# Group norm's chain spread over single-engine steps, fp8 rounding shared with GpSimd, and a searched start order

## The chip, the cores and the metric

The kernel runs on one NeuronCore of one Trainium2 chip. The metric is the device time of one execution in microseconds, the median of several runs. The engines are named as the profile names them: PE (matmul), PEld (its weight loads), DVE (VectorE), ACT (ScalarE), POOL (GpSimd) and SP (SyncE, which issues most DMAs here).

## The reference, cut to what matters

Two layers act on an image batch `x` of shape (4, 64, 64, 96). Layer 0 is a group norm over the image, a layer norm over the channels, one wide projection and a linear scan along the 4096 positions of each image, for 96 channels with 16 states each. Layer 1 is attention without a softmax (so that it collapses into one 96x96 matrix for each image) and a feed-forward net with values rounded to fp8 (e5m2) ahead of both products.

```python
x = x + conv(_gn(x))          # layer 0
t = t + attn(_ln_t(t))        # layer 1: (q k^T) v, no softmax
t = t + ffn(_ln_t(t))         # rounded to fp8 before each product

def _gn(v, G=32, eps=1e-5):   # 32 groups of 3 channels, over a whole image
    m = jnp.mean(g, axis=(1, 2, 4), keepdims=True)
    s = jnp.var(g, axis=(1, 2, 4), keepdims=True)
    return ((g - m) / jnp.sqrt(s + eps)).reshape(v.shape)

def step(h, ins):             # layer 0, over 4096 positions
    h_new = d * (A_t * h) + d * (B_t * u_t[..., None])
    y = g_t * jnp.sum(C_t * h_new, axis=-1)
```

## The kernel before, in words

Each of the 4 images is cut into 8 chunks of 512 positions, and each chunk's 1536 rows of state into 12 tiles of 128 partitions. That makes 384 tiles, numbered k, and the main loop (L1401 to L1424) makes one **step** s for each. In step s it emits, in this order: for tile s+3 the projection B on PE (`b_proj`, three matmuls, L269) and its copy out of PSUM on ACT (`b_copy`, L811); the projections A of tile s+1 and C of tile s on PE; `keep` on ACT; the product `b_mul` of tile s+2 on POOL (L814); on some tiles `c_mul_pool` of tile s-1 on POOL (L863); on DVE the scan of tile s (L830), `a_mul` of tile s+1 (L823) and `c_mul` of tile s (L854). Then it emits what `call(s)` finds in a table of other work for this step. Engines run what they are given in the order in which it was emitted, each engine for itself, and wait for one another through semaphores. Projection B has one PSUM bank, A two, and the small products share three banks named M.

The table is filled by `at(step, fn)`. The offsets of a chunk's pieces are in the dictionary `AT`. `front` puts the layer norm and the projections of the next chunks there, `tail` and `ffn` the second layer of earlier ones, and `group_norm` the statistics of the next image: `sums` and `sums_out` for its 8 chunks, and then a chain of small pieces. `moments` (L579) is two DVE and three POOL instructions; `mean` (L588) is a matmul, two DVE instructions and two on POOL; `root` (L600) is a matmul, one DVE instruction and one on POOL; `diagonal` (L608) is on ACT; `spread` (L616) is a matmul, and `spread_out` (L623) an ACT copy of the result to all partitions. `make` (L632) opens the group norm of an image with `first` (L561), a transpose and ACT instructions (L564, L566); image b's `make` is in step 6 for b = 1, in step 63 for b = 2 and in step 159 for b = 3, so the next image's `make` falls near the end of an image's chain. The last `sums` of images 1, 2 and 3 are in steps 57, 149 and 245.

Before step 6 and after step 383 the order comes from a small **planner** (class `Plan`, L412). A `job` has an engine, a cost in microseconds, a function that emits its instructions and the jobs it comes after. The planner places jobs by time and rank; with `tries` above zero it repeats that with random changes of rank and keeps the order whose `late` value is the lowest. It only fixes the order in which instructions are emitted; on the chip the instructions wait for their real inputs. `planned_start` (L1222) plans the first nine tiles and the normalization of the first two chunks, with `tries` at 0. The plan `end` (L888, 800 tries) orders what is left after the last step: the second layer of the last image and the last feed-forward chunks of the image before it, 11 chunks' feed-forward in all.

In the end a feed-forward chunk goes through `attention` (PE), `residual` and `stats` (DVE), `rstd` (POOL, L378 and L392), `apply` (ACT at L396, or DVE at L403 where `vector` is set), `transpose` (PE), `quant_in` (ACT, L1098), three `hidden` (PE, L1102) with `round_hidden` (ACT, L1119) and `relu_vector` (DVE, L1123), `quant` (ACT, L1127: 128x1536 values from fp16 to fp8), `project_out` (PE, L1133), `round_out` (ACT at L1143 or DVE at L1141), `bias_out` and `total` (POOL at L1148 and L1155, or DVE), and `store` (SP).

## Time and profile before

| what | value |
|---|---|
| median of 3 runs | 1183.2 us (1182.86 to 1183.66) |
| the profiled execution's own time | 1184.49 us |
| its span, first to last instruction | 1182.8 us |
| busy: PE, DVE, POOL, ACT | 1140.1, 1113.2, 1030.3, 817.3 us |
| first scan begins (tile 0) | 34.74 us |
| scan of tile 6 begins (first step of the loop) | 53.34 us |
| last scan begins (tile 383) | 1108.38 us |

The span is 1.69 us shorter than the time of that execution, and that execution is 1.29 us above the median. A line of a timeline reads: start, duration, engine, source line, operation, output and input with their sizes, count, and in brackets the idle time of the engine just before, with the instruction that ended it. A merged line (x4) covers several instructions in a row. A line of the table by stretches gives the stretch, its length, the busy time of each engine with its count of instructions, the granted PE clock, the busy share of the DMA engines and GB/s.

### The profile page before, as it was taken

To read this page: it belongs to the slowest core of one execution; us is meant where nothing else is said; L and a number is where in the kernel's file an instruction comes from. 1 tells how busy PE (TensorE), PEld (TensorE's weight loads), DVE (VectorE), ACT (ScalarE), POOL (GpSimd) and SP (SyncE) were. 2 spreads that over 40 slices of the span, in tenths; PEclk is the share of its full clock that TensorE was granted. 3 is DMA by queue.
4 is the path that set the end of the run, shared out by engine and by line. 5 is a ranking of instruction groups with operands and counts; after the bars stand their busy time and mean duration, and the time that the engine had idled before them with its cause. 6 is when DMAs were issued, how large, how long until landed. Compare 5 with 4: busy or idle time off the path is not lost. (4 is left out here: it accounts for less than half of the span.)

```text
span 1182.8 us, 19203 instructions
## 1 busy us (share of the span) xinstructions
PE 1140.1 (96%) x5899; PEld 874.6 (74%) x5899; DVE 1113.2 (94%) x2093; ACT 817.3 (69%) x1826; POOL 1030.3 (87%) x1176
## 2 busy tenths in 40 slices
PE   5999999999999999999999999999999999999885
PEld 4777777677777777777777777777777777777573
DVE  6999999899999999999999999999999999999865
ACT  4666655556556777877877777777776777776476
POOL 5798887788889899999999999999999999988554
PEclk8999999899999999999999999999999999999989
DMA  7676776687776776787777777766777778667221
GB/s 185 142 167 143 167 155 154 141 176 161 170 160 151 161 162 157 158 190 170 161 159 161 172 162 166 171 158 152 159 165 169 160 162 185 147 145 153 60 75 47
DMA packets 104288, 182.12 MB, mean 154 GB/s; under 512 B 42637, under 2 KB 50769, under 8 KB 104186
## 3 DMA queue, kind: packets, MB, share of 16 engines
q1 hardware_dynamic: 90060, 106.96, 37.3%
q0 software_dynamic: 13536, 73.93, 31.4%
q8 instruction: 46, 0.75, 0.3%
q14 instruction: 56, 0.46, 0.1%
q10 hardware_dynamic: 590, 0.02, 0.0%
HBM read 69.12 MB, written 24.77 MB: 79 GB/s over the span
## 5 line engine op out<-in xcount | busy, mean ns | idle before, releaser
L814 POOL TENSOR_TENSOR bu<-bu,rep 128x512 f32<-128x512 f32 x384 | 512.9, 1345 | 43.3 <-ACT state L840 34.8
L830 DVE TENSOR_TENSOR_SCAN h<-Aps,state,bu 128x512 f32<-128x512 f32 x336 | 426.2, 1268 | 0.7 <-POOL ch L863 0.5
L811 ACT ACTIVATE bu<-Bps,b_bac 128x512 f32<-128x512 f32 x384 | 263.1, 685 | 198.5 <-PE Bps L269 192.9
L823 DVE SCALAR_TENSOR_TENSOR Aps<-Aps,b_bac,rep 128x512 f32<-128x512 f32 x384 | 281.9, 734 | 8.2 <-PE Aps L269 8.2
L269 PE MATMUL Bps<-xs,w 128*128 128x512 f32 x768 | 268.0, 430 | 7.7 <-ACT bu L811 7.1
L269 PE MATMUL Aps<-xs,w 128*128 128x512 f32 x768 | 242.2, 396 | 1.2 <-DVE h L830 1.0
L863 POOL TENSOR_TENSOR ch<-ch,h 128x512 f32<-128x512 f32 x126 | 170.4, 1352 | 7.9 <-ACT ch L860 3.7
L269 PEld LDWEIGHTS Aps<-xs,w 128*128 128x128 f32 x768 | 143.9, 188 | 37.3 <-DVE h L830 3.0
L269 PEld LDWEIGHTS Bps<-xs,w 128*128 128x128 f32 x768 | 126.7, 191 | 51.2 <-ACT bu L811 15.4
L269 PE MATMUL Aps<-xl,w 128*128 128x512 f32 x384 | 152.0, 396 | 0.0
L269 PE MATMUL Bps<-xl,w 128*128 128x512 f32 x384 | 151.7, 395 | 0.0
L269 PE MATMUL Dps<-xs,w 128*128 128x512 f32 x384 | 121.0, 396 | 0.0
L269 PE MATMUL Cps<-xs,w 128*128 128x512 f32 x384 | 120.6, 395 | 0.0
L854 DVE SCALAR_TENSOR_TENSOR ch<-Dps,b_bac,h 128x512 f32<-128x512 f32 x160 | 118.6, 742 | 0.9 <-PE Dps L269 0.5
L869 POOL DMA_DIRECT2D ch<-ch x94 | 89.6, 953 | 0.3 <-DMA ch<-ch 0.3
L269 PEld LDWEIGHTS Bps<-xl,w 128*128 128x128 f32 x384 | 72.5, 189 | 17.7
L269 PEld LDWEIGHTS Dps<-xs,w 128*128 128x128 f32 x384 | 72.3, 188 | 17.7
L269 PEld LDWEIGHTS Aps<-xl,w 128*128 128x128 f32 x384 | 72.2, 188 | 17.7
L269 PEld LDWEIGHTS Cps<-xs,w 128*128 128x128 f32 x384 | 72.0, 188 | 17.6
L860 ACT ACTIVATE ch<-Cps,b_bac 128x512 f32<-128x512 f32 x94 | 64.6, 688 | 24.1 <-PE Cps L269 24.1
L269 PE MATMUL Dps<-xl,w 128*128 128x512 f32 x192 | 75.9, 395 | 0.0
L269 PE MATMUL Cps<-xl,w 128*128 128x512 f32 x192 | 75.8, 395 | 0.0
(200 smaller groups left out, 2045.2 us busy)
## 6 DMA issues: line engine op xcount, KB each, us to landing
ch<-ch POOLq DMA_DIRECT2D x94, 768.0 KB, 6.7
rep<-ddd SPq DMA_DIRECT2D x124, 384.0 KB, 7.4
ddd<-dd SPq DMA_DIRECT2D x31, 384.0 KB, 3.2
xl<-lo SPq DMA_DIRECT2D x62, 128.0 KB, 2.5
x<-in_x_dram SPq DMA_DIRECT2D x32, 192.0 KB, 3.0
xatd<-xat SPq DMA_DIRECT2D x32, 192.0 KB, 3.6
xal<-xatd SPq DMA_DIRECT2D x32, 192.0 KB, 2.8
out_dram<-o SPq DMA_DIRECT2D x32, 192.0 KB, 2.1
```

What stands on the lines that cost most here:

```text
L269: nc.tensor.matmul(ps, lhsT=wt[:, n], rhs=mv, start=(n == 0), stop=(n == 2))
L811: nc.scalar.activation(self.bu, self.b_ps, AF.Identity, bias=self.bias(0))
L814: nc.gpsimd.tensor_tensor(self.bu, self.bu, rep[self.b, self.i][:, 1, self.cg], ALU.mult)
L823: nc.vector.scalar_tensor_tensor(self.a_ps, self.a_ps, self.bias(1), rep[self.b, self.i][:, 0, self.cg], ALU.add, ALU.mult,)
L830: nc.vector.tensor_tensor_scan(self.h, self.a_ps, self.bu, 0.0 if self.i == 0 else state[self.sh, self.cg], ALU.mult, ALU.add,)
L854: nc.vector.scalar_tensor_tensor(self.slot(), self.c_ps, self.bias(2), self.h, ALU.add, ALU.mult)
L860: nc.scalar.activation(self.ch, self.c_ps, AF.Identity, bias=self.bias(2))
L863: nc.gpsimd.tensor_tensor(self.ch, self.ch, self.h, ALU.mult)
L869: nc.gpsimd.dma_start(chs[g, 0], chs.pop((g, sh)), accum_op=ALU.add)
```

## The change

Six edits. **Group norm's chain**: `moments`, `mean` and `root` are cut into seven pieces (`moments`, `variances`, `group_sums` twice, `mean`, `squares`, `offset`, `root`), each of which issues to one engine, and the eleven pieces of the whole chain are put one a step from the step after the last `sums_out`; before, the chain lay in 5 steps, with the last piece 8 steps after the last `sums`, and now it ends 12 steps after it. **Weights**: the four `weights_` functions emit their PE transposes in one step and their DVE copies in the next. **The end**: `quant` runs on POOL for chunks with i % 3 other than 0; `round_out` runs on ACT for all chunks; `apply` runs on DVE for i % 4 == 0 where it was i % 2 == 0 (last image); 1500 tries. **The fetch** of image 2's last chunk goes from step K - 4 to K - 1. **The second chunk's centring** on POOL comes after the first split (`low`) on POOL, where it waited for a time mark. **The start** is searched, with 800 tries, for a low weighted sum of end times: half the weight on the last planned scan, half on the second chunk's read, 0.01 on every other job.

```diff
--- before.py
+++ after.py
@@ -334,23 +334,26 @@
     def weights_attention():
         ps = bank("M", [C, CA], "wq_ps")
         nc.tensor.transpose(ps, w_qkv[:, 0:C], ident[:CA, :CA])
-        nc.vector.tensor_copy(w_qt[0:C, :], ps)
+        return lambda: nc.vector.tensor_copy(w_qt[0:C, :], ps)
 
     def weights_ffn1():
         ps = bank("M", [C, HID], "w1_ps")
         for m in range(NK):
             nc.tensor.transpose(ps[:, m * P : (m + 1) * P], w1_sb[:, m, :], ident)
-        nc.vector.tensor_copy(w1_q, ps, saturate=False)
+        return lambda: nc.vector.tensor_copy(w1_q, ps, saturate=False)
 
     def weights_ffn2():
         ps = bank("M", [P, NK, C], "w2_ps")
         for m in range(NK):
             nc.tensor.transpose(ps[:, m, :], w2_sb[:, m * P : (m + 1) * P], ident[:C, :C])
-        nc.vector.tensor_copy(w2_q, ps, saturate=False)
+        return lambda: nc.vector.tensor_copy(w2_q, ps, saturate=False)
 
     def weights_bias():
         ps = bank("M", [P, NK], "b1_ps")
         nc.tensor.transpose(ps, b1_sb, ident[:NK, :NK])
+        return lambda: biases_out(ps)
+
+    def biases_out(ps):
         b1_8 = small.tile([P, NK], F8, tag="b1_8", name="b1_8", bufs=1)
         nc.vector.tensor_copy(b1_8, ps, saturate=False)
         nc.vector.tensor_copy(b1_q, b1_8)
@@ -520,7 +523,9 @@
                 self.time[e] = t + j["cost"]
 
         def late(self, starts):
-            return max(t + self.jobs[n]["cost"] for n, t in starts.items())
+
+            ends = [(t + self.jobs[n]["cost"], self.jobs[n].get("weight", 0.0)) for n, t in starts.items()]
+            return sum(t * w for t, w in ends) or max(t for t, _ in ends)
 
     steps = {}
 
@@ -580,29 +585,45 @@
             t = small.tile([C, 2], F32, tag="gt", name=f"gt_{self.b}", bufs=2)
             nc.vector.tensor_reduce(t, self.s, AX.X, ALU.add)
             nc.vector.tensor_scalar_mul(t, t, 1.0 / L)
+            self.t = t
+
+        def variances(self):
+            t = self.t
             nc.gpsimd.tensor_tensor(self.mv[:, 0:1], t[:, 0:1], self.c, ALU.subtract)
             nc.gpsimd.tensor_tensor(t[:, 0:1], t[:, 0:1], t[:, 0:1], ALU.mult)
             nc.gpsimd.tensor_tensor(self.mv[:, 1:2], t[:, 1:2], t[:, 0:1], ALU.subtract)
 
 
+        def group_sums(self, name):
+            self.ps = bank("M", [C, 2], f"g{name}_ps_{self.b}")
+            nc.tensor.matmul(
+                self.ps[:, 0:1], lhsT=third, rhs=self.mv[:, 0:1] if name == "m" else self.w,
+                start=True, stop=True,
+            )
+
         def mean(self):
-            ps = bank("M", [C, 2], f"gm_ps_{self.b}")
-            nc.tensor.matmul(ps[:, 0:1], lhsT=third, rhs=self.mv[:, 0:1], start=True, stop=True)
+            ps = self.ps
             self.m = small.tile([C, 2], F32, tag="gm", name=f"gm_{self.b}", bufs=2)
             nc.vector.tensor_copy(self.m[:, 0:1], ps[:, 0:1])
             w = small.tile([C, 1], F32, tag="gw", name=f"gw_{self.b}", bufs=2)
             nc.vector.tensor_tensor(w, self.mv[:, 0:1], ps[:, 0:1], ALU.subtract)
-            engine = nc.gpsimd if self.b else nc.vector
+            self.w = w
+
+        def squares(self):
+            w, engine = self.w, nc.gpsimd if self.b else nc.vector
             engine.tensor_tensor(w, w, w, ALU.mult)
             engine.tensor_tensor(w, w, self.mv[:, 1:2], ALU.add)
-            self.w = w
+
+        def offset(self):
+            self.v = small.tile([C, 1], F32, tag="gv", name=f"gv_{self.b}", bufs=2)
+            nc.vector.tensor_scalar(self.v, self.ps[:, 0:1], 1e-5, None, ALU.add)
 
         def root(self):
-            ps = bank("M", [C, 2], f"gv_ps_{self.b}")
-            nc.tensor.matmul(ps[:, 0:1], lhsT=third, rhs=self.w, start=True, stop=True)
-            v = small.tile([C, 1], F32, tag="gv", name=f"gv_{self.b}", bufs=2)
-            nc.vector.tensor_scalar(v, ps[:, 0:1], 1e-5, None, ALU.add)
-            nc.gpsimd.tensor_tensor(self.m[:, 1:2], v, mhalf[0:C, 0:1], ALU.pow)
+            nc.gpsimd.tensor_tensor(self.m[:, 1:2], self.v, mhalf[0:C, 0:1], ALU.pow)
+
+        def all_of(self, *pieces):
+            for name, *args in pieces:
+                getattr(self, name)(*args)
 
 
         def diagonal(self, k0=0, k1=2):
@@ -649,9 +670,12 @@
                 at(max(when[n] - 7, when[n - 1]), load_gx, b, n)
             at(when[n], call, "sums", n)
             at(when[n] + AT["sums_out"] - AT["sums"], call, "sums_out", n)
-        for n, name in ((1, "moments"), (2, "mean"), (4, "root"), (6, "diagonal"), (8, "spread"),
-                        (8, "spread_out")):
-            at(when[-1] + n, call, name)
+        chain = (
+            ("moments",), ("variances",), ("group_sums", "m"), ("mean",), ("squares",),
+            ("group_sums", "v"), ("offset",), ("root",), ("diagonal",), ("spread",), ("spread_out",),
+        )
+        for n, args in enumerate(chain):
+            at(when[-1] + AT["sums_out"] - AT["sums"] + 1 + n, call, *args)
 
 
     split, rep, gate = {}, {}, {}
@@ -891,7 +915,7 @@
         {"ACT": 0.5, "DVE": 2.5, "POOL": 1.5},
     )
     end.last = {}
-    end.tries = 800
+    end.tries = 1500
 
     def place(plan, s0):
 
@@ -1064,7 +1088,7 @@
         def tile_of(tag, drain_tag, shape, dtype, name):
             return sb(drain_tag if phase["end"] else tag, shape, dtype, f"{name}_{nm}")
 
-        vector = b == B - 1 and i % 2 == 0
+        vector = b == B - 1 and i % 4 == 0
 
         def fetch():
             v["xa"] = next_of(xal_t, "xal")
@@ -1124,7 +1148,10 @@
 
         def quant():
             v["hq"] = sb("bu", [P, NK, TC], F8, f"hq_{nm}")
-            nc.scalar.activation(v["hq"], v["h16"], AF.Copy, saturate=False)
+            if i % 3 == 0:
+                nc.scalar.activation(v["hq"], v["h16"], AF.Copy, saturate=False)
+            else:
+                nc.gpsimd.tensor_copy(v["hq"], v["h16"], saturate=False)
 
         def project_out():
             ps = v["ps"] = bank("A" if phase["end"] else "M", [P, J, C], f"y2_ps_{nm}")
@@ -1137,10 +1164,7 @@
 
         def round_out():
             v["y16"] = tile_of("y16", "xs", [P, J, C], F16, "y16")
-            if phase["end"] and i % 2:
-                nc.vector.tensor_copy(v["y16"], v["ps"])
-            else:
-                nc.scalar.copy(v["y16"], v["ps"])
+            nc.scalar.copy(v["y16"], v["ps"])
 
         def bias_out():
             last_two = phase["end"] and b == B - 1 and i > NCH - 3
@@ -1170,7 +1194,7 @@
         )
         done = place(plan, s0)
         if fetch not in done and b < B - 1:
-            at(K - 4, fetch)
+            at(K - 1, fetch)
             done.add(fetch)
         if store in done:
             return
@@ -1203,10 +1227,10 @@
                         free=[f"h:{nm}"] if m == 2 else [])
                 c = job("ACT", 0.57, round_hidden, m, after=[h, c],
                         take=[f"rep:{nm}"] if m == 0 else [], free=[f"M:{m}{nm}"])
-                r.append(job("DVE", 0.5, relu_vector, m, after=[c]))
-            a = job("ACT", 1.5, quant, after=r, take=[f"bu:q{nm}"], free=[f"rep:{nm}"])
+                r.append(job("DVE", 0.47, relu_vector, m, after=[c]))
+            a = job(*(("ACT", 1.5) if i % 3 == 0 else ("POOL", 1.6)), quant, after=r, take=[f"bu:q{nm}"], free=[f"rep:{nm}"])
         a = job("PE", 0.5, project_out, after=[a], take=[f"A:y{nm}"], free=[f"bu:q{nm}"])
-        a = job(*(("ACT", 0.48) if vector else ("DVE", 0.56)), round_out, after=[a],
+        a = job("ACT", 0.48, round_out, after=[a],
                 take=[f"xs:{nm}"], free=[f"A:y{nm}"])
         last_two = b == B - 1 and i > NCH - 3
         a = job(*(("DVE", 0.6) if last_two else ("POOL", 0.95)), bias_out, after=[a], take=[f"xl:{nm}"], free=[f"xs:{nm}"])
@@ -1243,8 +1267,8 @@
         b = mm(0.8, bias_turn, after=[b], key="M:b")
         b = job("DVE", 0.35, bias_out, after=[b], free=["M:b"])
         a = job("DVE", 0.4, q.aggregate, after=a)
-        m = job("DVE", 1.1, q.mean, after=[a])
-        r = job("DVE", 0.7, q.root, after=[m], late=0.9)
+        m = job("DVE", 1.1, q.all_of, ("group_sums", "m"), ("mean",), ("squares",), after=[a])
+        r = job("DVE", 0.7, q.all_of, ("group_sums", "v"), ("offset",), ("root",), after=[m], late=0.9)
         g = []
         for n, a in enumerate((m, r)):
             a = job("ACT", 0.37, q.diagonal, n, n + 1, after=[a, *g])
@@ -1260,6 +1284,7 @@
         wd = job("SP", 1.0, split_copies, w_dug[:, 0], w_dug[:, 1], w_dug[:, 2], after=[ld], late=2.2)
         wr = [job("ACT", 0.45, repeat, n, k, after=[(hd, ld)[n]]) for n in range(2) for k in range(2)]
         w = {"rep": job("SP", 1.0, split_copies, *(w_rep[:, n] for n in range(3)), after=wr, late=2.2)}
+        first_low = None
         for sh in range(NSH):
             plan.rank = 3 * sh - 3
             for k in range(3):
@@ -1270,6 +1295,7 @@
                     plan.rank = 1 if k == 0 else 3 * sh - 3
                     t = job("POOL", 1.3, low, k, sh, nc.gpsimd, after=[t, calm])
                     low_b = t if k == 0 else low_b
+                    first_low = first_low or t
                 v = w_bac[k][:, :, :, sh * P : (sh + 1) * P]
                 w[k, sh] = job("SP", 1.0, split_copies, *(v[:, n] for n in range(3)), after=[t], late=2.4)
         plan.rank = -4
@@ -1325,7 +1351,7 @@
 
 
         plan.rank = 1
-        a = job("POOL", 1.0, second.centre, nc.gpsimd, after=[*g, calm])
+        a = job("POOL", 1.0, second.centre, nc.gpsimd, after=[*g, first_low])
         a = job("POOL", 1.0, second.scale, nc.gpsimd, after=[a])
         a = job("DVE", 1.1, second.stats, after=[a])
         a = job("POOL", 1.8, second.ln.rstd, after=[a])
@@ -1345,7 +1371,7 @@
         b = mm(0.7, second.proj, 0, after=[a], key="M:u2")
         a = job("DVE", 0.74, second.du_out, after=[a, b], free=["M:u2"])
         a = job("SP", 0.5, second.write, after=[a], late=3.4)
-        job("SP", 1.8, second.read, after=[a])
+        read = job("SP", 1.8, second.read, after=[a])
         plan.rank = 6
         job("SP", 0.5, load_gx, 1, 0, after=[land("free0", 34.0)])
         job("SP", 4.0, load_late, after=[land("free1", 37.0)])
@@ -1362,13 +1388,22 @@
                 awake[0][:, 0:P], lhsT=ident, rhs=ident, start=True, stop=True
             )
 
+
+        for j in plan.jobs:
+            j["weight"] = 0.01
+        for j in (s, read):
+            j["weight"] = 0.5
+        plan.tries = 800
         plan.run(stay_awake)
         return second
 
     second = planned_start()
 
+    def turned(step, fn):
+        at(step + 1, fn())
+
     for n, fn in enumerate((weights_attention, weights_ffn1, weights_ffn2, weights_bias)):
-        at(NT + 8 + NT * n, fn)
+        at(NT + 8 + NT * n, turned, NT + 8 + NT * n, fn)
     for b in range(B):
         for i in range(NCH):
             g = b * NCH + i
```

## The prediction

> **What bounds the kernel now.** I read the busy shares first, then the busy times by stretch, then the timelines of single engines where DVE or PE stands idle.
>
> ```profile
> PE 1140.1 (96%) x5899; PEld 874.6 (74%) x5899; DVE 1113.2 (94%) x2093; ACT 817.3 (69%) x1826; POOL 1030.3 (87%) x1176
> ...
> 53.34:1108.40 1055.06, 1044.17 (x5307) 804.11 (x5305) 1025.38 (x1849) 740.26 (x1690) 963.64 (x1074) 1.00 0.73 160
> 1108.40:1125.50 17.10, 15.26 (x110) 9.77 (x110) 11.71 (x48) 8.78 (x18) 6.57 (x12) 1.00 0.23 67
> 1125.50:1142.00 16.50, 16.48 (x97) 13.40 (x97) 10.53 (x48) 9.72 (x17) 8.80 (x15) 0.69 0.29 86
> 1142.00:1174.20 32.20, 23.62 (x201) 16.18 (x198) 21.39 (x75) 30.67 (x52) 17.09 (x24) 1.00 0.18 49
> ```
>
> The columns are PE, PEld, DVE, ACT, POOL, then PE's clock. In the loop (first stretch) DVE and PE run level. Adding up every idle time in DVE's timeline between 44 and 1107 us gives 28.4 us, of which 17.1 is one wait of 0.2 to 1.0 us in each chunk (L926, for `o_ps`), which no edit touches. In the last stretch ACT is busy 30.67 of 32.20 us: there ACT is the bound, and POOL has 15 us free. Between these two lies a latency chain (last scan, gram matrix, attention matrix at 1125.4).
>
> The largest stop in the loop is at image 1's group norm, on ACT:
>
> ```profile
> 212.07 1.54 ACT L396 ACTIVATE z<-z,nmr_c,rstd_c 128x96 f32<-128x96 f32 x4 [1.53 <-POOL nmr_c L384]
> 213.51 0.63 ACT L612 ACTIVATE gdg<-ident,gm 96x96 f32<-96x96 f32 x2
> 214.05 0.58 ACT L564 ACTIVATE gc_ps<-gc_ps 96x512 f32<-96x512 f32 x1
> ...
> 214.88 0.67 ACT L811 ACTIVATE bu<-Bps,b_bac 128x512 f32<-128x512 f32 x1
> ```
>
> on PE:
>
> ```profile
> 215.61 1.22 PE L269 MATMUL Bps<-xs,w 128*128 128x512 f32 x2 [2.56 <-ACT bu L811]
> ```
>
> and on DVE:
>
> ```profile
> 218.57 0.76 DVE L823 SCALAR_TENSOR_TENSOR Aps<-Aps,b_bac,rep 128x512 f32<-128x512 f32 x1 [2.42 <-PE Aps L269]
> ```
>
> A late layer norm, the group norm's diagonal (L612) and the next image's `make` (L564) meet in step 63. They hold back the copy L811 that frees PE's only B bank; PE stands 2.56 us and then works at half speed:
>
> ```profile
> 216.00:221.00 5.00, 5.00 (x16) 3.98 (x15) 2.06 (x4) 1.08 (x3) 2.57 (x3) 0.50 0.78 191
> ```
>
> [...] Here 2.56 us was enough (clock 0.50), while 1.90 us of idle PE at 1144.08 left the next stretch at 1.00; the measurement decides. [...] L403 takes 0.32 us undisturbed, and up to 1.22 us in the start beside POOL (below).
>
> **The change, part by part.** The sum is made against the profiled execution, 1184.49 us (span 1182.8), which is 1.29 above the median; I subtract the same sum from the median 1183.2.
>
> *Group norm, image 1.* DVE's idle times at 214.87, 218.57, 219.85 and 223.03 are 0.53 + 2.42 + 0.52 + 1.24 = 4.71 us. The diagonal moves from step 63 to 67, which takes 0.55 us (start to start, L612 to L564) out of ACT's burst. `root` (0.58 us on POOL, L605) leaves step 61, so the layer norm's rstd and then L396 begin about 0.55 earlier. The copy L811 starts at 214.88 - 1.1 = 213.8. Against that, `squares` (0.47 + 0.19) now stands in step 63 on POOL behind L814 and L863: 213.58 + 1.26 - 0.58, so 214.25 to 214.9. `group_sums` v waits for it on PE in step 64, ahead of the next B matmul. PE thus stands from 213.05 to 214.9, some 1.9 us in place of 2.56, and `a_mul` comes at about 216.9 in place of 218.57: 1.7 saved. If the clock holds, the later waits (0.52 and 1.24) shrink to 0.4: 3.0 in all. If it drops again, 1.0 is saved. With 7 to 3 for the clock holding: **-2.4** (bounds 0 and -4.7).
>
> *Images 2 and 3.* Each has two small stops (0.37 + 0.49; 0.37 + 0.48), because POOL waits 0.58 us at L605 for DVE ahead of another layer norm's rstd, and the diagonal lies ahead of L811 at 469.34. Both move away. The new place of image 2's diagonal is step 149 + 10 = 159, which is where image 3's `make` is: the same three ACT pieces as at 213. There, at 481.61, L811's copy ends at 483.12 and the next B matmul starts at 483.17, so 0.55 more on ACT goes on to PE; I book +0.5. Image 3's diagonal (step 255) meets no `make`: +0.1. Sum: -0.86 - 0.85 + 0.6 = **-1.1** (-1.7 to +3.1).
>
> *Weights.* The four DVE copies (L337, L343, L349, L355) wait for nothing in this trace, so parting them from PE saves **0**; an M bank is held a step longer, at most 0.3 us each.
>
> *Fetch.* In SP's timeline image 2's last two fetches (L1071) start at 1077.5 and about 1086, and nothing else stands between them; attention needs them at 1111.4. The edit swaps the two in SP's queue, and so which of two buffers each takes: **0**. The first fetches of image 3 then wait for the other of two attentions, which follow each other within 1.9 us; the matrix that those chunks need comes only at 1125.4, which covers that.
>
> *Start.* DVE's chain to the first scan is stretched where POOL centres the second chunk.
>
> ```profile
> 21.12 3.31 DVE L403 TENSOR_SCALAR z<-z,mv_c,rstd_c 128x96 f32<-128x96 f32 x4 [0.17 <-POOL rstd_c L392]
> 24.35 2.47 DVE L259 TENSOR_TENSOR w<-raw,w 128x384 fp32r<-128x384 f32 x2
> ```
>
> on POOL:
>
> ```profile
> 21.03 1.03 POOL L670 TENSOR_TENSOR z<-x,gmr 128x384 f32<-128x384 f32 x1
> 22.14 1.08 POOL L673 TENSOR_TENSOR z<-z,gmr 128x384 f32<-128x384 f32 x1
> ```
>
> Four L403 alone take 4 x 0.32 = 1.28; 2.0 us is contention. Now a split comes first on POOL. It needs its ACT cast, the fifth or sixth of six ending at 22.1, so it starts near the end of the apply and leaves most of it undisturbed: up to -2.0. But a split is also a two-input POOL instruction and, started early, would disturb as much: 0. The search can win DVE's idle time, 3.38 us between 16 and 53 minus the part before 20: 2.1 at most; or lose some, since its costs know no contention. I take **-1.5** (+1.5 to -4).
>
> *End.* A cast on ACT (L1127) costs 11.6 / 8 = 1.45 us net. Of the eight in the ACT-bound stretch five go to POOL (i = 1, 2, 4, 5, 7): -7.25. Back onto ACT come five `round_out` at 0.48 (L1141 after 1142): +2.4, and `apply` of i = 2 and 6 at 1.5 (L396): +3.0. ACT's 30.67 becomes 28.8. Each `round_out` now makes ACT wait for PE's L1133, with `round_hidden` copies queued behind it, which `relu_vector` on DVE waits for; before, ACT waited 0.9 us there in all, so I book nothing and leave 0.9 in the range. DVE only gets lighter. The cast on POOL is not in the trace in this form; two rows bound it.
>
> ```profile
> L208 POOL CAST ident<-ident x1: 291/291/291, 5.3 to 5.3; 128x128 fp8e5<-128x128 f32 x1
> ...
> L1148 POOL TENSOR_TENSOR yb<-y,b_q x30: 910/921/973, 415.5 to 1174.2; 128x384 f16<-128x384 f16 x30
> ```
>
> A one-element POOL instruction (L583) takes 0.188. The cast's slope is (0.291 - 0.188) / 128 = 0.80 ns, hence 0.188 + 1536 x 0.80 ns = 1.42 us. The two-input slope, (0.921 - 0.188) / 384 = 1.91 ns, gives 3.12. [...] I take 1.5: POOL becomes 17.09 + 5 x 1.5 + 2 x 0.5 (nmr of two chunks) = 25.6 of 30 us, still below ACT. Behind a cast in POOL's queue stand rstd and `total` of other chunks; ACT's apply waits for rstd. The planner can place it, at a cost in latency that ACT's backlog hides. I take ACT's saving, rounded: **-2.0** (+8 to -4).
>
> Sum: -2.4 - 1.1 - 1.5 - 2.0 = -7.0. The profiled execution would be 1177.5, the median 1183.2 - 7.0 = **1176.2**.
>
> **The rivals.**
> 1. *Freed ACT time is not used*: the last stretch is a chain of eight chunks, and PE and DVE waited there too (DVE 5.0 us for L1133). End 0: 1178.2. For: ACT already has 0.9 us of waits for xq. Against: 95% busy.
> 2. *The stop moves to image 2*: with the diagonal in step 159, PE idles over 2 us, the clock drops, and image 1's old 4.7 us stand there in place of the 0.5 booked: 1176.2 + 4.2 = 1180.4. For: the same three pieces. Against: PE waited under 0.1 us there before.
> 3. *The cast on POOL costs 3.1 us* and POOL bounds the end; this ends **slower**. POOL: 17.09 + 1.0 + 15.6 = 33.7 us, +1.5 over the stretch's 32.2; the last cast ends 1.7 later; two rstd stand behind a cast for half of it, +3.2; three relus of the last chunk beside casts at 0.9 in place of 0.35, +1.6. End +8.0: 1183.2 - 5.0 + 8.0 = 1186.2. POOL overtakes ACT from (28.8 - 18.1) / 5 = 2.1 us a cast, and the whole is slower from about 3 us.
> 4. *The searched start is worse on the chip*, +2 where I have -1.5: 1179.7.
>
> **How the numbers follow.** Forecast 0.55 (own range 1171.5 to 1180.5), rivals 0.15, 0.12, 0.10, 0.08. A measurement of this kernel can tell about 0.2% from no change: faster is below 1180.8, slower above 1185.6. Faster: 0.53 + 0.14 + 0.06 + 0.06 = 0.79 (rival 2 lies at the bound and counts half); same 0.02 + 0.01 + 0.06 + 0.01 + 0.01 = 0.11; slower 0.10, nearly all of it rival 3. The range is 1170.5 to 1183.5: it takes in rivals 1, 2 and 4 and leaves out rival 3.
>
> **What would show it.** Group norm right: no wait above 1.5 us on DVE near 218, PE's clock 1.00 there, and no idle PE above 1 us in step 159 (478 to 482 us now). Start right: the first L403 four under 1.6 us, first scan before 33.5. End right: casts on POOL at 1.4 to 1.7 us, ACT's busy time after the last scan down by 2 to 4 us, last scan to end of span (74.4 us now) down by 2. Wrong: casts above 2.1 us, PE's clock at 0.5 anywhere between 200 and 490, or the first scan later than 34.7.

## The result, and the profile after

The change made no difference that can be measured: 1183.84 us (median of 4, 1181.86 to 1185.16) against 1183.03 on the same chip, ratio 1.0006 [0.9988, 1.0025]. The prediction was 1176.2. The profiled execution took 1182.68 us, span 1181.0. From the page of after:

```profile
PE 1137.2 (96%) x5882; PEld 871.3 (74%) x5882; DVE 1115.4 (94%) x2079; ACT 813.6 (69%) x1833; POOL 1040.5 (88%) x1187
```

The busy times by stretch, cut as for the kernel before (the loop, last scan to attention matrix, and the two parts of the rest; columns PE, PEld, DVE, ACT, POOL, PE's clock):

```profile
53.64:1103.73 1050.09, 1041.95 (x5308) 801.93 (x5306) 1025.28 (x1847) 739.87 (x1690) 963.41 (x1074) 1.00 0.73 161
1103.73:1123.16 19.43, 15.69 (x107) 10.90 (x107) 13.54 (x47) 9.03 (x20) 8.55 (x13) 0.91 0.21 60
1123.16:1139.70 16.54, 15.85 (x105) 12.83 (x105) 10.47 (x53) 11.19 (x25) 10.70 (x19) 0.80 0.32 91
1139.70:1171.90 32.20, 22.76 (x163) 14.47 (x163) 22.42 (x58) 25.08 (x50) 24.12 (x30) 0.89 0.17 47
```

The loop took 4.97 us less (1055.06 before). The stretch to the attention matrix took 2.33 more (17.10 before). In the stretch of 32.2 us, which ends about 9 us before the span does, ACT fell from 30.67 to 25.08, and no time came of it.

Scan by scan, after against before: tile 12 is 0.69 later (start), tiles 62 to 70 take 23.07 in place of 27.71 (group norm, image 1), tiles 149 to 170 take 59.51 in place of 60.05, tiles 245 to 262 take 48.64 in place of 49.17. The last scan is 4.65 earlier, but from it to the end of the span 77.27 us pass in place of 74.42. Before, then after, from the last scan to the end of the span:

```profile
1108.38:1182.80 74.42, 55.60 (x403) 39.44 (x403) 45.91 (x172) 49.17 (x86) 34.57 (x52) 0.90 0.21 61
```

```profile
1103.73:1181.00 77.27, 54.99 (x386) 38.73 (x386) 48.14 (x158) 46.16 (x93) 45.51 (x63) 0.85 0.21 59
```

**Group norm, after.** Line numbers are 3 to 24 higher than before. On ACT, image 1:

```profile
211.50 1.54 ACT L399 ACTIVATE z<-z,nmr_c,rstd_c 128x96 f32<-128x96 f32 x4
212.95 0.57 ACT L569 ACTIVATE gc_ps<-gc_ps 96x512 f32<-96x512 f32 x1
...
213.79 0.67 ACT L835 ACTIVATE bu<-Bps,b_bac 128x512 f32<-128x512 f32 x1
```

On PE, and the stretch that had a clock of 0.50 before:

```profile
214.78 0.33 PE L599 MATMUL gv_ps<-gw,third 96*96 96x1 f32 x2 [0.80 <-POOL gw L615]
214.97 0.71 PE L269 MATMUL Bps<-xs,w 128*128 128x512 f32 x2
```

```profile
216.00:221.00 5.00, 5.00 (x26) 3.20 (x25) 4.55 (x8) 2.85 (x8) 4.75 (x5) 1.00 0.83 184
```

The apply no longer waits for POOL, the diagonal is gone from between it and L569, and the copy starts at 213.79. PE then waits for `squares` on POOL, but only 0.80 us, and keeps its clock.

**Start, after.** On DVE, and on POOL:

```profile
21.15 3.30 DVE L406 TENSOR_SCALAR z<-z,mv_c,rstd_c 128x96 f32<-128x96 f32 x4 [0.16 <-POOL rstd_c L395]
```

```profile
21.08 1.19 POOL L259 TENSOR_TENSOR w<-raw,w 128x384 fp32r<-128x384 f32 x1
22.22 1.01 POOL L694 TENSOR_TENSOR z<-x,gmr 128x384 f32<-128x384 f32 x1
23.30 1.08 POOL L697 TENSOR_TENSOR z<-z,gmr 128x384 f32<-128x384 f32 x1
```

The split took the centring's place beside the apply, which is as slow as before (3.31). And there is a wait that the kernel before didn't have, on PE for the second chunk's low part and so on DVE:

```profile
48.80 0.44 PE L269 MATMUL dug_ps<-xl,w_dug 128*96 128x512 f32 x1 [0.50 <-DMA xl<-lo]
```

```profile
50.75 0.75 DVE L737 SCALAR_TENSOR_TENSOR dd<-dug_ps,b_dug,dd 96x512 f32<-96x512 f32 x1 [1.11 <-PE dug_ps L269]
```

**End, after.** The first group is all casts on POOL, the second the last image's `apply` in `tail` (the columns after the count are minimum/median/maximum in ns, then first and last start):

```profile
L1154 POOL CAST hq<-h x7: 1461/1464/1499, 1114.6 to 1170.4; 128x1536 fp8e5<-128x1536 f16 x7
...
L406 DVE TENSOR_SCALAR xa<-x,mv_a,rstd_a x4: 318/320/1452, 1114.6 to 1116.5; 128x96 f32<-128x96 f32 x4
```

The cast costs what was predicted (1.46 us, 1.5 taken). But the first of them runs from 1114.56 to 1116.02, and of the four instructions beside it one took 1452 ns in place of 320, as long as the cast. The last gram matrix waits for them, and PE, idle for 1.77 us, goes on at half speed (clock 0.50):

```profile
1116.14 1.59 PE L968 MATMUL gram_ps<-xa 128*97 128x97 f32 x8 [1.77 <-DVE xa L406]
```

```profile
1117.00:1118.00 1.00, 1.00 (x8) 0.97 (x7) 0.51 (x3) 0.00 (x0) 0.00 (x0) 0.50 0.00 0
```

Later some relus and some of the `apply` on DVE take longer too, beside the casts and also beside POOL's additions (L1172, L1179). From the end of the kernel before and of after:

```profile
L1123 DVE TENSOR_SCALAR h<-h,b_q 128x512 f16<-128x512 f16 x33 | 12.9, 411 | 4.7 <-ACT h L1119 3.6
L403 DVE TENSOR_SCALAR xn<-x,mv_f,rstd_f 128x96 fp8e5<-128x96 f32 x16 | 6.0, 435 | 0.0
```

```profile
L1147 DVE TENSOR_SCALAR h<-h,b_q 128x512 f16<-128x512 f16 x33 | 17.0, 552 | 7.6 <-ACT h L1143 7.3
L406 DVE TENSOR_SCALAR xn<-x,mv_f,rstd_f 128x96 fp8e5<-128x96 f32 x8 | 5.7, 772 | 1.0 <-POOL rstd_f L395 1.0
```

(After the bar: busy us, mean ns of one, then the idle time ahead.) The relus went from 411 to 552 ns, the apply from 435 to 772. The casts are only a part of that: with no cast on POOL, another order of the kernel before (number 3 below) has relus of 482 ns.

### The profile page after: what moved, and what is told of

It is laid out like the page before. It is cut to its first block, busy times and chain, and to the rows that moved or that the text cites. A ratio compares the mean times of both kernels' runs of the same rounds, so it can differ in the third digit from the quotient of the medians.

```text
span 1181.0 us, 19185 instructions
## 1 busy us (share of the span) xinstructions
PE 1137.2 (96%) x5882; PEld 871.3 (74%) x5882; DVE 1115.4 (94%) x2079; ACT 813.6 (69%) x1833; POOL 1040.5 (88%) x1187
```

## The experiments

Differences are (ratio - 1) x 1183.3 us; each kernel ran beside the kernel before (medians there 1183.2 to 1183.6). "End" is the time from the last scan to the end of the span in the one profiled execution; six profiles of kernels with the end of before have 73.6 to 75.9 there. "Planner" is the end time that the kernel's own planner computes for the order it keeps.

### The change in its parts

Group norm's pieces alone:

```diff
-        for n, name in ((1, "moments"), (2, "mean"), (4, "root"), (6, "diagonal"), (8, "spread"),
-                        (8, "spread_out")):
+        for n, args in enumerate(chain):
+            at(when[-1] + AT["sums_out"] - AT["sums"] + 1 + n, call, *args)
```

> The kernel before with the group norm's chain of the change alone. Theory A (the parts add, and group norm's gain was real but spent elsewhere): the loop ends 5.3 us earlier as in the trace of the changed kernel (4.3 at image 1, 0.5 at each of images 2 and 3), start and end as before, so 1183.0 - 5.3 = 1177.7. Theory B (the gain at image 1 came from another state of the loop, left by the new start): PE still idles over 2 us near step 64 and under 2 us are saved, 1181 or more.

All of the end's edits and the fetch, nothing else:

```diff
+                nc.gpsimd.tensor_copy(v["hq"], v["h16"], saturate=False)
...
-        vector = b == B - 1 and i % 2 == 0
+        vector = b == B - 1 and i % 4 == 0
...
-            if phase["end"] and i % 2:
-                nc.vector.tensor_copy(v["y16"], v["ps"])
```

> The kernel before with the end's edits alone (fp8 cast on GpSimd for i % 3 other than 0, round_out on ACT, apply on DVE for i % 4 == 0, 1500 tries, the later fetch). Both theories of the end expect it slower by what the trace of the changed kernel shows from the last scan to the end, 71.3 us against 68.4: +2.9, so 1185.9. If the end is not slower here (within 0.7 of before), the loss in the changed kernel depends on where the loop leaves the engines.

The same with every cast left on ACT:

```diff
-            if i % 3 == 0:
-                nc.scalar.activation(v["hq"], v["h16"], AF.Copy, saturate=False)
-            else:
-                nc.gpsimd.tensor_copy(v["hq"], v["h16"], saturate=False)
+            nc.scalar.activation(v["hq"], v["h16"], AF.Copy, saturate=False)
...
-            a = job(*(("ACT", 1.5) if i % 3 == 0 else ("POOL", 1.6)), quant, after=r, take=[f"bu:q{nm}"], free=[f"rep:{nm}"])
+            a = job("ACT", 1.5, quant, after=r, take=[f"bu:q{nm}"], free=[f"rep:{nm}"])
```

> As the end's edits alone, but with every fp8 cast on ACT as before (round_out on ACT, apply on DVE for i % 4 == 0, 1500 tries, the relu's planned cost of 0.47, the later fetch are kept). Theory 1 (the cast on GpSimd stretches DVE's tensor_scalar instructions beside it, and the first one lies in the chain to the attention matrix): without it the matrix is ready 17.1 us after the last scan as before, not 19.4; ACT now carries 5.4 us more than before in the ACT-bound stretch, so this kernel is slower than before too, by 3 to 5 us, but with L403 at 0.3 us each. Theory 2 (the new order of the plan is what is late, whichever engine casts): the matrix stays late, over 18.5 us after the last scan.

The start alone (search and centring):

```diff
+        plan.tries = 800
...
-        a = job("POOL", 1.0, second.centre, nc.gpsimd, after=[*g, calm])
+        a = job("POOL", 1.0, second.centre, nc.gpsimd, after=[*g, first_low])
```

> The kernel before with the start's edits alone (searched order, the second chunk's centring behind the first split). The trace of the changed kernel has tile 6's scan 0.3 us and tile 12's 0.7 us later than before, so +0.7: 1183.7. If the searched order were a gain that the other edits hide, tile 12's scan would begin before 68.9.

Measured: group norm 0.9970 [0.9958, 0.9982], **-3.6**; end 1.0028 [1.0016, 1.0040], **+3.3**; end without casts on POOL 1.0003 [0.9995, 1.0011], +0.4; start 1.0009 [1.0002, 1.0016], **+1.1**. The three parts sum to +0.8, which is what the whole shows (1183.84 - 1183.03). So group norm's gain is real and is given back by two of the other edits, mostly the end.

Group norm alone also shows a loss that nobody had booked. `moments` in its new step runs beside POOL's second centring instruction, and its DVE instruction L582, which takes 0.17 us before, takes 1.11. On POOL, then on DVE:

```profile
200.66 1.15 POOL L692 TENSOR_TENSOR z<-z,gmr 128x384 f32<-128x384 f32 x1
```

```profile
200.74 1.11 DVE L582 TENSOR_SCALAR gt<-gt 96x2 f32<-96x2 f32 x1
```

Tiles 55 to 62 take 21.38 us there and 20.63 in the kernel before. Both combined kernels at the end of this section have it too (1.12 and 1.14 us); in after POOL came later to that instruction, and L587 took 0.17.

The end without the casts was expected to lose 3 to 5 us, and lost nothing that can be measured. Its window from the last scan to the end of the span:

```profile
1106.75:1181.30 74.55, 55.07 (x388) 37.84 (x387) 41.30 (x158) 54.70 (x100) 34.73 (x56) 0.86 0.22 61
```

ACT carries 54.70 us where the kernel before has 49.17, in the same 74.5 us. So this end had room on ACT for 5.5 us more, though the order is another one as well. Beside it, after has 8.5 us less on ACT (46.16), 6.8 more on DVE (48.14 against 41.30), and is 2.7 longer. Not all of the 6.8 comes from the casts. An estimate from the trace of after: its `tensor_scalar` instructions of over 0.5 us took 11.5 us more than 0.33 us each would have, 5.1 of them beside a cast and 6.4 beside POOL's additions; before has 3.8, all beside the additions.

### The pieces of the group norm and of the start

Only the last three pieces moved, to the steps that the change gives them; the rest of the chain is whole, as before:

```diff
-        for n, name in ((1, "moments"), (2, "mean"), (4, "root"), (6, "diagonal"), (8, "spread"),
-                        (8, "spread_out")):
+        for n, name in ((1, "moments"), (2, "mean"), (4, "root"), (10, "diagonal"), (11, "spread"),
+                        (12, "spread_out")):
```

> The kernel before with only the group norm's diagonal, spread and spread_out moved 4 steps on (steps 67, 68, 69 for image 1), the other pieces left. If the diagonal in ACT's burst is the larger part of the stop: PE idles 2.0 us in place of 2.56 at image 1 and runs on at full clock, and the two small waits of images 2 and 3 shrink only in part; the gain is 2 to 3 us of the whole chain's 3.6: 1181. If the wait of GpSimd for DVE in root is the larger part, less than 1 us is gained: 1182.6 or more.

Measured: 0.9998 [0.9988, 1.0007]. The diagonal leaves ACT's burst, but the apply still waits for POOL, where `root` stands ahead of another layer norm. On ACT, then PE:

```profile
213.55 1.55 ACT L396 ACTIVATE z<-z,nmr_c,rstd_c 128x96 f32<-128x96 f32 x4 [1.54 <-POOL nmr_c L384]
215.01 0.58 ACT L564 ACTIVATE gc_ps<-gc_ps 96x512 f32<-96x512 f32 x1
```

```profile
216.56 0.79 PE L269 MATMUL Bps<-xs,w 128*128 128x512 f32 x2 [2.05 <-ACT bu L811]
```

PE's stop shrinks from 2.56 to 2.05 us, near the 0.55 that the prediction booked for the diagonal, and PE's clock is still 0.66 in the 5 us after it. Only with the other half too, `root` out of the layer norm's way, is the stop on ACT gone: in group norm alone PE waits 1.20 us, for POOL.

The centring behind the first split, without the search; then the search without the moved centring:

```diff
-        a = job("POOL", 1.0, second.centre, nc.gpsimd, after=[*g, calm])
+        a = job("POOL", 1.0, second.centre, nc.gpsimd, after=[*g, first_low])
```

> The kernel before with the second chunk's centring planned behind the first GpSimd split, and no search. Theory A (GpSimd's split disturbs the first apply as much as the centring did): four L403 still take 3.3 us, the first scan is at 34.7 and the time is that of before, 1183.4 within 0.3; the start's +0.9 then comes from the searched order. Theory B (the swap itself delays the second chunk): +0.9.

```diff
+        for j in plan.jobs:
+            j["weight"] = 0.01
+        for j in (s, read):
+            j["weight"] = 0.5
+        plan.tries = 800
```

> The start's order searched with its weights, without the moved centring. By difference (search and centring together +1.1 us, centring alone -1.1) the search costs +2.2: 1185.8, and the last of the first image's tiles follow some 0.8 us later than in the kernel before, from tile 12 on. If the loss came from the two together, the search alone is at 1183.6 +/- 0.6.

Measured: centring 0.9990 [0.9981, 0.9999], -1.2; search 1.0000 [0.9989, 1.0010]. The centring fits neither of its two theories: the apply takes 3.30 us as expected, but a little time is gained (the interval almost reaches 1), and where it comes from is not known. The +2.2 that I expected of the search from the difference isn't there; only the two together cost. The search alone has the new wait of PE for the DMA too (0.64 at 48.40, and DVE 1.14 at 50.34), and tiles 0 to 12 take 34.63 us, with the centring 34.99, in after 35.02, in the kernel before 34.20. Fourteen profiles of programs with the start of before have 34.19 to 34.61 there, with the first scan between 34.3 and 36.5 us, so one profile can't price the search alone; the pair's 0.8 stands out. The new waits are not shown to be the cause: the search alone has them too, and its time is that of before.

### The end: where the cast stands

Both kernels keep all other edits of the end. In the first, the cast goes to POOL for the last image only, and the order is searched anew. In the second, the order is the one of the change, job for job, but image 2's two casts in the end are issued on ACT:

```diff
-            a = job(*(("ACT", 1.5) if i % 3 == 0 else ("POOL", 1.6)), quant
+            a = job(*(("ACT", 1.5) if i % 3 == 0 or b < B - 1 else ("POOL", 1.6)), quant
...
-            if i % 3 == 0:
+            if i % 3 == 0 or b < B - 1:
```

> The end's edits alone, with the fp8 cast on GpSimd only for the last image's chunks 1, 2, 4, 5 and 7; image 2's three chunks cast on ACT, and the plan is searched with that. Theory 1 (the loss is the GpSimd cast beside DVE's L403 in the chain to the attention matrix): the matrix is ready 17.1 us after the last scan in place of 19.3 and the stretch after it stays near 52, so about 2.3 less than the end's edits alone: 1183.8. Theory 2 (the order that the search finds with GpSimd casts is late): the matrix stays later than 18.5 us.

```diff
-            if i % 3 == 0:
+            if i % 3 == 0 or b < B - 1:
```

> The end's edits alone, in exactly their order: the plan still books image 2's casts on GpSimd, but they are issued on ACT at the same place of the order. Theory 1 (contention of the cast with DVE's L403): with the order unchanged, L403 of the last tail takes 1.05 us for its four in place of 2.2, and the matrix is ready by 17.9 us after the last scan in place of 19.3. Theory 2 (the order): L403 may shorten, but the matrix stays at 19 us, because what stands ahead of the gram sum on DVE and PE is the same.

Measured: 0.9959 [0.9946, 0.9972], **-4.9**, and 1.0015 [1.0005, 1.0026], +1.8. The second is the clean pair with the end alone (+3.3): same order, and only the engine of two instructions differs. The apply is whole again, PE waits 0.65 us, and the eight matmuls behind that wait take 1.13 us, as they do in the kernel before, where the clock from 1120 to 1125 was 1.00 (in the end alone 1.45, after a wait of 1.78):

```profile
L403 DVE TENSOR_SCALAR xa<-x,mv_a,rstd_a x4: 328/330/331, 1117.8 to 1118.5; 128x96 f32<-128x96 f32 x4
```

```profile
1118.19 1.13 PE L944 MATMUL gram_ps<-xa 128*97 128x97 f32 x8 [0.65 <-DVE xa L403]
```

The matrix is ready 16.34 us after the last scan, where the end alone took 19.28: of the 2.94, 1.12 is the apply (2.17 to 1.05) and the rest PE, slower after the longer wait, and what waits for it. PE's next four matmuls (L931) took 1.06 us in the end alone, as in after at a clock of 0.50, and 0.64 here. The medians lie 1.5 us apart, and their intervals overlap, so this pair is clear in the trace and not in the times. And it explains neither why the first of the two gains 4.9, nor why the second is still 1.8 slower than before. I had expected neither.

The third keeps the order that gained 4.9 and takes the cast away: the five casts, planned on POOL, are issued on ACT.

```diff
-            if i % 3 == 0 or b < B - 1:
+            if True:
```

> The order that the search found for the cast on POOL in the last image alone, but those five casts issued on ACT as well; nothing else differs. Theory 'ACT's lighter load pays': ACT gets 5 x 1.47 = 7.3 us back in a stretch where it idles 11 us, so at least half of the -4.9 is lost, 1181.5 to 1185. Rival 'it is the order (relus first, residuals early), not the cast': 1179 to 1180.5.

Measured: 0.9997 [0.9990, 1.0003], -0.4. The two intervals don't touch. So in this order the five casts on POOL are worth 4.5 us, 0.9 each, and the theory "ACT's lighter load pays" holds there. From the last scan to the end of the span, this kernel and then the one with casts on POOL:

```profile
1108.66:1182.40 73.74, 56.54 (x383) 38.47 (x382) 41.59 (x158) 54.46 (x100) 34.89 (x56) 0.82 0.22 62
```

```profile
1107.44:1177.30 69.86, 53.29 (x383) 36.72 (x382) 44.54 (x158) 48.00 (x95) 42.49 (x61) 0.84 0.23 65
```

ACT loses 6.5 us of work and the stretch 3.9. The first cast there starts at 1142.27, long after the matrix (1124.04).

### The end: what the order is worth

The planner's search begins from a random number. Nothing but that number is changed here, in the end with both images' casts on POOL, in the end with the last image's alone, and in the kernel before.

```diff
-            rng = random.Random(1)
+            rng = random.Random(3)
```

> All of the end's edits, casts on POOL for two of three chunks of both images, the search begun from another random number (the planner's own end time 64.4 us, 63.7 with the first). Theory 'the cast stands ahead of the last image's matrix': the third image's casts on POOL cost the matrix 2 to 3 us in any order, so 1185 to 1187 again and the matrix more than 18.5 us after the last scan. Rival 'luck of the order': what the search finds differs on the chip by several us for nothing in the edit; 1180 to 1187, the matrix at 16.5 to 17 as likely as at 19.

> The cast on POOL for the last image's chunks alone, the search begun from another random number (the planner's own end time 65.4, 66.0 with the first). Theory 'ahead of the matrix': with no cast there the gain stays, 1179 to 1180.5, matrix at 16.5 to 17. Rival 'luck of the order': the -4.9 us was a draw; between 1179 and 1185, most likely near 1182.

and with `random.Random(2)`:

> All of the end's edits with another random number for the search (planner's own end time 65.5 us). Theory 'casts of both images cost': last scan to last DVE 69.5 to 71.5 us, as with the first two (71.5, 69.6), and 1184.5 to 1186. Rival 'luck of the order': 65 to 71 us, 1179 to 1186.

> The cast on POOL for the last image alone, another random number (planner's own end time 65.1 us). Theory 'casts of both images cost, of the last alone pay': last scan to last DVE 65 to 66.5 us as with the first two (65.3, 65.8), 1179 to 1181.5. Rival 'luck of the order': 65 to 71 us, 1179 to 1186.

> The kernel before with nothing changed but the random number of the end's search (planner's own end time 67.1 us, 69.1 before). What the order alone is worth: if the planner's own time counts, 2 us less, 1181.5; if it only redraws the order, anything from 1181 to 1186.

and the kernel before with `random.Random(3)`:

> The kernel before with a third random number for the end's search (planner's own end time 69.9 us; 69.1 for the first, 67.1 for the second). If the planner's own time ranks the orders: 1183 to 1184.5. If the first order was merely a poor draw and most are better: 1177 to 1181. If the second was a rare good one: 1182 to 1186.

| end of | number | planner, us | end, us | ratio | difference |
|---|---|---|---|---|---|
| before | 1 | 69.1 | 74.4 | 1 | 0 |
| before | 2 | 67.1 | 67.7 | 0.9942 [0.9931, 0.9954] | -6.9 |
| before | 3 | 69.9 | 73.7 | 1.0002 [0.9993, 1.0012] | +0.2 |
| edits, all casts on ACT | 1 | 71.7 | 74.6 | 1.0003 [0.9995, 1.0011] | +0.4 |
| edits, casts of both images (the change) | 1 | 63.7 | 77.5 | 1.0028 [1.0016, 1.0040] | +3.3 |
| same | 2 | 65.5 | 71.7 | 0.9983 [0.9975, 0.9990] | -2.0 |
| same | 3 | 64.4 | 75.5 | 1.0015 [1.0008, 1.0022] | +1.8 |
| edits, casts of the last image | 1 | 66.0 | 69.9 | 0.9959 [0.9946, 0.9972] | -4.9 |
| same | 2 | 65.1 | 68.7 | 0.9949 [0.9937, 0.9960] | -6.0 |
| same | 3 | 65.4 | 71.8 | 0.9988 [0.9979, 0.9997] | -1.4 |

The order alone is worth up to 6.9 us, more than any part of the change. Two results lie below all that I had expected of them: before with number 2 (1177.14 us, 1181 to 1186 expected) and the last image's casts with number 2 (1177.86, 1179 at the lowest). The kernel before with the second number, no cast on POOL and the same work on ACT:

```profile
1109.20:1176.90 67.70, 50.30 (x394) 34.95 (x394) 45.64 (x172) 49.52 (x86) 34.22 (x52) 0.95 0.24 67
```

ACT is busy 49.52 us, as before (49.17), in 6.7 us less. The two profiles show where ACT's idle time went. In the 16.5 us after the attention matrix ACT is busy 15.04 here; in the kernel before it was 9.72 (third line of the prediction's table by stretch; 9.8 to 12.1 in the six profiles with that end, counted from the end of the matrix). In the last 8.6 us of the span it is busy 2.08, and in those six not at all. This order, then before:

```profile
1126.38:1142.88 16.50, 14.06 (x123) 11.02 (x124) 12.53 (x59) 15.04 (x30) 11.43 (x20) 1.00 0.38 109
1168.30:1176.90 8.60, 2.82 (x19) 2.02 (x17) 1.24 (x3) 2.08 (x3) 1.84 (x2) 0.70 0.25 69
```

```profile
1174.20:1182.80 8.60, 0.24 (x6) 0.09 (x3) 2.26 (x3) 0.00 (x0) 2.11 (x2) 0.69 0.17 46
```

So ACT gets its work earlier and keeps it to a later point; the same end in the second combined kernel below has 15.04 and 2.12. Both pure theories fall. "The cast ahead of the matrix costs in any order" fails with the second number, where no cast meets the apply (1.05 us) and the same edits gain 2.0; with the third it meets the apply (2.17 us) and yet the matrix comes after 16.05 us. "All luck" doesn't fit the pair of equal order with the last image's casts. And the planner's own time doesn't rank the orders across the forms: of all ten, the one that it rates best is the slowest on the chip. Within a form it ranks the three of before rightly and the three with both images' casts the wrong way round.

### The parts that gained, together

Group norm, the centring without the search, and the end with the last image's casts on POOL; then group norm, the centring and the end of the kernel before with the second number:

```diff
-            rng = random.Random(1)
+            rng = random.Random(2)
```

> The parts that gained, together: group norm's pieces, the second chunk's centring behind the first split with no search of the start, and the end's edits with the cast on POOL for the last image alone. If the parts add as they did in the whole change: 0.9970 x 0.9959 x 0.9990 = 0.9919, 1174.0 us for a kernel before of 1183.6. If the end's gain was a lucky order that only fits the state in which the kernel before leaves the engines, or if the parts share a gain: 0.994 to 0.996, 1176.5 to 1179.

> Group norm's pieces, the second chunk's centring behind the first split, and the end of the kernel before in the order from the second random number: no cast on POOL at all. If the parts add (0.9970 x 0.9990 x 0.9942 = 0.9902): 1171.7 us for a kernel before of 1183.3. If the order of the end gained only beside the start and middle it was drawn with: 1175 to 1178.

Measured: 0.9939 [0.9927, 0.9952], 1175.57 us, and 0.9919 [0.9904, 0.9934], **1173.94 us** against 1183.27. Both are faster than either kernel. Both fall some 2 us short of the product of their parts (0.9919 and 0.9902), which is within what the parts' intervals allow. The best version has no cast on POOL.

## Why the prediction was wrong, step by step

- **Group norm, -3.5 predicted, -3.6 measured.** Right, and in the main by its mechanism: copy at 213.79 (213.8 said), PE waiting for `squares` until 214.78 (214.9 said), clock held at 1.00. That the instants agree so closely is luck, since tile 62 began 0.78 us later than before; PE stood 0.80 us (1.20 in group norm alone) where 1.9 were booked. Tiles 62 to 70 took 27.71 us in the profile of before, but 26.2 to 26.4 in thirteen of the fourteen later profiles that leave group norm alone (the same stop, 2.53 to 2.59 us, with a clock of 0.61 to 0.73 after it). Against those they gain some 3.3 us, near the 3.0 of the branch in which the clock holds. But in group norm alone about 0.8 goes back at L582, which the prediction had left out, and 0.3 at tiles 71 and 72, so image 1 gives some 2.2 net (tiles 58 to 72: 39.46 us in group norm alone, 41.5 to 41.8 in those thirteen), beside the 2.4 booked. Images 2 and 3 give 0.5 each, 1.1 together as booked. The sum is right because its errors cancel. Rival 2, the stop in step 159, didn't come.
- **Weights and fetch, 0.** The fetch was tried only with the end, the weights not at all; the sum of the parts leaves nothing for them, to within some 3 us.
- **Start, -1.5 predicted, +1.1 measured.** My two bounds were +1.5 and -4, and the sentence "a split ... would disturb as much: 0" was the one that held: the apply took 3.30 after 3.31. The search won nothing by itself, and together with the centring it costs; by what, the runs don't show. It went the way of rival 4.
- **End, -2.0 predicted, +3.3 measured: the step that failed.** Three sentences of it. "There ACT is the bound": ACT was busy 95% of the stretch of 32.2 us, but only 9.72 of the 16.5 us before it, and not at all in the 8.6 us after it. With 5.5 us more on ACT (and a new order) the end took no longer, and with the same load in another order 6.7 less. The stretch was full because the order had piled the work up there. The forecast for ACT itself came true, down by 3.0 us over the end (2 to 4 said), and the end grew by 2.8: freed ACT time was not used, as rival 1 had it, and more was lost. That doesn't mean that ACT's load is without weight: with the order held, 6.5 us less on ACT brought 4.5. "DVE only gets lighter": over the end DVE was busy 48.14 us (45.58 in the end alone) after 45.91, although six `round_out` (3.3 us) had left it; some 5 us of it are time beside casts (the estimate above). "The planner can place it, at a cost in latency that ACT's backlog hides": the planner put the first cast beside the one DVE instruction that the attention matrix waits for, where there is no backlog, and the matrix came 2.3 us later. The price of the cast, 1.5, was right (1.46); rival 3 (3.1 us) was not the reason. The size of the step could not be had from the profile at all: 1500 tries draw a new order, and new orders of the same work lie up to 7 us apart. I had given that no range of its own.

The trace of before shows what I left unused: over its end a relu takes 0.32 to 0.90 us and an `apply` on DVE 0.30 to 0.98, the seven of over 0.5 us each beside one of POOL's additions (L1148 and L1155, 0.92 and 0.95 us in the mean). I booked such a stretch for the start and, in rival 3, for three relus, but not in the forecast of the end or for group norm's small pieces. In after, of the four applies the one that started just after a cast of 1.46 us took 1452 ns, the other three 318 to 320.

**What stays open.** Why the search finds an order that keeps ACT at work in one draw and not in the next, and what sets the time in the orders with casts. PE's clock doesn't tell it: over the end it is 0.95 in the best order of the kernel before (67.7 us), but 0.94 in one that takes 73.7, and 0.85 in one of the casts' (68.7). Nor does ACT's load over the end (49.5, 49.1 and 48.1). Three draws of each form (means -2.2 for before, +1.0 and -4.1 for the two cast forms) are too few to rank the forms, since draws of one form lie up to 7 us apart.

## What to carry to other kernels

Where an order comes out of a random search over a cost model, an edit to its jobs is also a new draw: measure both sides over several draws before believing either, and judge by the chip, not by the model's own time. A high busy share of an engine in a stretch shows a bound only if a lighter or heavier load on it moves the end of that stretch. Look at the stretches on both sides too: an engine that is full in one and idle in the next may have its queue in a bad order. Before work is moved to GpSimd, or DVE work to another step, look for the instructions that will lie beside each other, and who waits for the DVE one: here one of 0.32 us took 1.45 beside a cast, and one of 0.17 took 1.11 beside a centring.

## What was not expected of the hardware

A cast of 128x1536 from fp16 to fp8 took POOL 1.46 us, and a DVE instruction of 0.32 us that began just after it took 1.45 (end of after); a DVE instruction of 0.17 us on 96x2 values took 1.11 beside a POOL instruction of 1.15 (group norm alone). PE idle for 1.77 us ran at 0.50 for some 3 us afterwards (end of after), while 2.35 us near tile 64 (start alone) left the next 5 us at 1.00, 2.56 us there gave 0.50 (before) and 2.53 gave 0.66 (search alone): the length of the stop alone doesn't tell the clock.
